# One core, a transformer block with routing: the last batch's outputs tile by tile, its last denominators in halves, its gates in the output weights

## The chip, the cores and the metric

The kernel runs on one core of one Trainium2 chip. The metric is device time in microseconds (us). The kernel before took 3617.36 us, the median of three runs that lay between 3617.17 and 3618.96 us.

## The reference, cut to what matters

The input x holds 8 batches of 1024 tokens with 256 features. A small matrix product of another input gives each batch six vectors of 256 numbers (sa, ca, ga, sb, cb, gb). All arithmetic is f32. In the reference's order:

```
ga = (2 * (ga >= 0) - 1) * maximum(abs(ga), 0.25)      # gb likewise
h  = layernorm(x) * (1 + ca) + sa
q, k, v of 16 heads of 64 features; softmax(q k' / 8) v; joined heads @ w_o
x  = x + ga * attention
h  = layernorm(x) * (1 + cb) + sb
logits = h @ router_w + router_b; scores = softmax over 8 experts
each expert takes the 512 tokens of all 8192 with its highest scores
h1 = relu(toks @ w1 + b1); eo = h1 @ w2 + b2; x = x + gb * (eo * score), added at the tokens
```

An expert cannot choose before the scores of all 8192 tokens are there. So everything after the attention of the last batch, up to its scores, lies ahead of the choice.

## The kernel before, in words

**Units.** Attention is cut into 128 units (NSU). Unit u is a batch b, a pair p of heads (8 pairs, NP) and a half h of the 512 queries (QB); the last two units, 126 and 127, are the two halves of the last pair of batch 7. A unit has 8 chunks c of 128 keys. For each chunk TensorE makes the scores (`scores_mm`, L367), ScalarE copies them to an SBUF tile with the tag "p" (16 buffers, L376), VectorE keeps a running maximum (L381) and later subtracts it (`subtract`, L426), ScalarE takes the exponential (`exp_of`, L429), and TensorE multiplies with the values (`values_mm`, L438); `values_out` (L447) copies the sum into the tile oT of the pair.

**Denominators.** GpSimd adds the eight chunks of a unit into one tile (`add_up`, L454 and L457), then TensorE sums that tile over its partitions with a matrix of ones (`den_mm`, L473), ScalarE copies the result (`den_store`, L481) and SyncE's queue carries it to DRAM. `den_load` fetches the two halves of a pair in a flat shape (L494), `den_inv` takes the reciprocal on VectorE (L499) and stores it (L501), `den_spread` spreads it over the partitions with two DMAs (L510), and `den_mul` multiplies oT with it (L517 or L519). For unit 127 alone no GpSimd addition is made: TensorE sums each of its eight chunks directly, in between the value products, into pd_last.

**Order.** The program is written out by hand in steps g, four to a unit; each engine and each DMA queue carries out its instructions in program order. `at(g, where, f, ...)` files a function under a step and one of the places "load", "m1", "post", "pool" and "m2" of it; `run` calls them. Values lag scores by six steps (LAG), so unit 127 is in g = 514 to 517. The denominators of unit u come at 4u + 12 in "m2".

**The end of the attention.** After the loop the store, the load, the reciprocal and the spread of the last pair are issued in one go, for both halves (units 126 and 127) together, and after them on the same SyncE queue the loads of the vectors of the last batch (mods, L777) and of its x (xs, L782). Eight loads of the earlier pairs' attention (`last_load`, L644), 384 KB each, stand in steps 515 and 516.

```
        for t in range(NT):
            for p in range(NP - 1):
                ...
        den_mul(b, NP - 1)
        for t in range(NT):
            add_pair(t, NP - 1, at_hand[b, NP - 1][:, t * P : (t + 1) * P])
        for s in range(NT + 5):
            if s < NT:
                out_add(b, s, pos[s])
            if 1 <= s < NT + 1:
                out_norm(b, s - 1)
            ...
```

The output product of the last batch (L797) thus runs over the first seven pairs of all eight token tiles t, then over the last pair of all eight, and only then come the sums, norms and router steps of the tiles. Per tile `out_add` multiplies the product by the gate (L558), adds x (L559), stores the row, and takes the statistics (L116, L117). `rstd_of` takes the inverse deviation on GpSimd (L106, L108). `out_norm` subtracts and scales on VectorE (L571), then multiplies and adds on GpSimd (L572, L573). For two tiles at a time `out_turn` transposes on TensorE (eight half-wide products a pair of tiles, L585) with a copy on ScalarE (L590), `out_route` makes the logits (L600, L605, L607), `out_exp` the exponentials (L615), `out_score` the scores (L622, L623, L626), and `out_store` copies the scores into the table of all tokens on GpSimd (L633) and stores the rows (L634).

**After it.** The whole table of scores is transposed (L883) and copied (L887), a search in 15 steps finds each expert's threshold (L898 to L916), the positions are made, rows are gathered, and eight experts run.

Of the kernel before, what the change touches and what calls it, by code (L numbers as in the profile page):

```python
# [28 lines left out]
F32 = mybir.dt.float32  # L29
# [3 lines left out]
ALU = mybir.AluOpType  # L33
# [4 lines left out]
P = 128  # L38
# [4 lines left out]
def adaln_block(  # L43
# [203 lines left out]
    def at(g, where, f, *args):  # L247
        steps.setdefault((g, where), []).append((f, args))
# [219 lines left out]
    def den_mm(pd, src, start=True, stop=True):  # L468

        for j in range(2):  # L470
            for i in range(2):
                r = (2 * j + i) * 32
                nc.tensor.matmul(  # L473
                    pd[r : r + 32, :], ones[:, :32], src[:, j, i * QH : (i + 1) * QH],
                    start=start, stop=stop, tile_position=(0, r),
                )

    def den_store(u, pd):
        b, p, h = unit(u)
        den = small.tile([P, QH], F32, tag="den", name=f"den{u}", bufs=2)  # L480
        nc.scalar.copy(den, pd)  # L481
        if h == 0:
            den_d[b, p] = dram.tile([2, S], F32, name=f"den_d{b}_{p}")
        nc.sync.dma_start(
            den_d[b, p][:, h * QB : (h + 1) * QB].rearrange("j (i q) -> j i q", i=2),
            den[::32, :],
        )


    dens = {}  # L490
# [1 line left out]
    def den_load(b, p):  # L492
        dens[b, p] = small.tile([P, 2 * S // P], F32, tag="dq", name=f"dq{b}_{p}", bufs=2)
        nc.sync.dma_start(  # L494
            dens[b, p], den_d.pop((b, p)).rearrange("j s -> (j s)").rearrange("(p c) -> p c", p=P)
        )
# [16 lines left out]

    def den_mul(b, p):
        oT = oTs.pop((b, p))
        if (b, p) == (B - 1, NP - 1):
            nc.vector.tensor_mul(oT, oT, dens.pop((b, p)))  # L517
        else:
            nc.gpsimd.tensor_tensor(oT, oT, dens.pop((b, p)), ALU.mult)  # L519
        if (b, p) in at_hand:  # L520
            at_hand[b, p] = oT
        else:
            nc.sync.dma_start(oT_d[b][p], oT)


    o_x, o_h, o_t = {}, {}, {}
# [49 lines left out]
    def out_turn(pool, b, t, tag="mm"):  # L576

        n = f"{b}_{t}"
        pt = pool.tile([P, 2, KC, P], F32, tag=tag, name=f"pth{n}")
        for i in range(2):  # L580
            h2 = o_h[b, t + i]
            for k in range(KC):
                for m in range(2):
                    c0 = k * P + m * N
                    nc.tensor.matmul(  # L585
                        pt[m * N : (m + 1) * N, i, k, :], h2[:, c0 : c0 + N], ident,
                        start=True, stop=True,
                    )
# [47 lines left out]
    def gates(b):  # L636
        nc.sync.dma_start(
            rows_d[b * S : (b + 1) * S, ROW:], gb_d[b : b + 1, :].to_broadcast([S, D])
        )

    def last_load(t):
        b = B - 1
# [56 lines left out]
    for u in range(NSU):  # L699
        at(4 * u + 4, "m1", max_rows, u)  # L700
        if u < NSU - 1:
            at(4 * u + 12, "m2", den_out, u)
    for b in range(B):
        at(64 * b + 30, "load", gates, b)
    for i in range(2):
        at(2 + i, "m2", mod_rows, i)
    for t in range(NT):
        at(4 * NSU + (3 if t < NT // 2 else 4), "load", last_load, t)

    with tc.manual_schedule():  # L710
        first_loads()
        late_loads()
        mod_silu()
        ln_first(0)
        ln_first(1)
        ln_norm(0, 0)
        mod_columns()
        for t in range(2, NT // 2):
            ln_first(t)
            ln_norm(0, t - 1)  # L720
        ln_norm(0, NT // 2 - 1)
        for t in parts_of:
            nc.vector.memset(t, 0.0)

        nc.gpsimd.memset(steps_of, 0)
        nc.gpsimd.iota(steps_of[:, 14, :], pattern=[[1, 4]], base=0, channel_multiplier=0)
        for s in range(14):
            nc.vector.tensor_scalar(
                steps_of[:, s, :], steps_of[:, 14, :], 28 - 2 * s, None, op0=ALU.logical_shift_left
            )  # L730
        g = -1
        while g < 4 * NSU + LAG or steps:
            u, gm = divmod(g, 4)
            run(g, "load")
# [12 lines left out]
            run(g, "m1")  # L747
            run(g, "post")
            for uc in late:
                exp_of(*uc)  # L750
            u1, gm1 = divmod(g - LAG, 4)
            if 0 <= u1 < NSU:
                for c in (2 * gm1, 2 * gm1 + 1):
                    values_mm(u1, c)
                    if u1 == NSU - 1:
                        if c == 0:
                            pd_last = ps_s.tile([P, QH], F32, tag="s", name="pd_last")
                        den_mm(pd_last, probs.pop((u1, c)), start=(c == 0), stop=(c == NT - 1))
# [12 lines left out]
        b = B - 1  # L771
        den_store(NSU - 1, pd_last)
        den_load(b, NP - 1)
        den_inv(b, NP - 1)
        den_spread(b, NP - 1)
        mods[b] = work.tile([P, 3, D], F32, tag="mod", name=f"mod{b}", bufs=1)
        nc.sync.dma_start(  # L777
            mods[b].rearrange("p m d -> p (m d)"), mod_d[b : b + 1, :].to_broadcast([P, 3 * D])
        )
# [9 lines left out]
        for pool, tag, n in (  # L789
            (ps_s, "s", 2), (ps_b, "less", 2), (ps_m, "mm", 1), (ps_av, "av", 1), (ps_s, "s", 2)  # L790
        ):
# [3 lines left out]
        def add_pair(t, p, src):  # L795
            for m in range(2):
                nc.tensor.matmul(  # L797
                    pos[t][m * N : (m + 1) * N, :], src[:, m * N : (m + 1) * N],
                    wo[:, p, :], start=(p == 0), stop=(p == NP - 1),
                )  # L800

        for t in range(NT):
            for p in range(NP - 1):
                if p < NP - 2:
                    add_pair(t, p, o_t[b, t][:, p, :])
                else:
                    add_pair(t, p, at_hand[b, p][:, t * P : (t + 1) * P])
        den_mul(b, NP - 1)
        for t in range(NT):
            add_pair(t, NP - 1, at_hand[b, NP - 1][:, t * P : (t + 1) * P])  # L810
        for s in range(NT + 5):
            if s < NT:
                out_add(b, s, pos[s])
            if 1 <= s < NT + 1:
                out_norm(b, s - 1)
            if s % 2 == 0 and 2 <= s < NT + 2:
                out_turn(*((ps_s, b, 0, "s") if s == 2 else (ps_m, b, s - 2)))
            if s % 2 and 3 <= s < NT + 3:
                out_route(ps_b, b, s - 3, tag="less")
                out_exp(b, s - 3)  # L820
            if s % 2 == 0 and 4 <= s < NT + 4:
                out_score(b, s - 4)
                out_store(b, s - 4)
    assert not steps, sorted(steps)
    attn.close()

# [283 lines left out]
```

## Time and profile before

| what | value |
|---|---|
| median of three runs | 3617.36 us |
| the profiled execution's own time | 3616.66 us |
| its span | 3614.9 us |
| TensorE busy | 96% of the span |
| VectorE, GpSimd, ScalarE busy | 80%, 74%, 67% |
| last value product's copy of the attention (L447) starts | 3213.17 us into the span |
| last scores copied into the table (L633) | 3271.52 us, for 0.33 us |
| first gathered rows asked for (L1007) | 3345.61 us |

The profiled execution took 1.76 us more than its span. All times inside the span are counted from its start. In the timeline a row gives start, length, engine, line and operation, then what is written and read, and in brackets how long the engine sat idle and what released it. PEld is the weight load of TensorE, SPq the issuing of DMAs on SyncE's queue. The rows of TensorE count two or four hardware passes for one f32 product.

### The profile page before, as it was taken

How to read it: one execution, taken by the hardware profiler on the slowest of the kernel's cores; microseconds unless marked ns; L12 is line 12 of the kernel's file. 1: busy time of each engine (PE TensorE's matmuls, PEld its weight loads, DVE VectorE, ACT ScalarE, POOL GpSimd, SP SyncE). 2: the span in 40 equal slices, each digit the busy share in tenths (PEclk: the TensorE clock that was granted, in tenths of full speed). 3: DMA queues.
4: the chain of work that ended last, by engine and by line, in shares of the span. 5: the costliest groups of instructions: out<-in, count | busy, mean ns of one | idle time of the engine just before them, and what ended most of it. 6: DMA issues, size and time to landing. Idle time of an engine off the chain costs nothing. (4 is left out here: it accounts for less than half of the span.)

```text
span 3614.9 us, 54207 instructions
## 1 busy us (share of the span) xinstructions
PE 3458.4 (96%) x20622; PEld 1456.3 (40%) x20622; DVE 2898.9 (80%) x3641; ACT 2439.8 (67%) x2988; POOL 2660.0 (74%) x1537
## 2 busy tenths in 40 slices
PE   7999999999999999999999999999999999982898
PEld 3333333343433443344433434334334344342565
DVE  5888888888888888888888888888888888857442
ACT  4777777777777777777777777777777777730111
POOL 2778777887788887977888788877888877851332
PEclk9999999999999999999999999999999999995999
DMA  3010012011111113111211112011201112133332
GB/s 77 13 42 31 25 32 67 29 45 45 59 50 35 51 49 64 31 39 51 61 46 44 41 44 62 30 52 48 67 29 45 45 59 49 51 87 121 94 100 41
DMA packets 189652, 185.39 MB, mean 51 GB/s; under 512 B 48952, under 2 KB 167240, under 8 KB 189264
## 3 DMA queue, kind: packets, MB, share of 16 engines
q1 hardware_dynamic: 173616, 160.29, 15.5%
q0 software_dynamic: 7168, 12.72, 1.7%
q10 hardware_dynamic: 8608, 8.92, 0.8%
q8 instruction: 162, 2.65, 0.3%
q14 instruction: 98, 0.80, 0.1%
HBM read 127.06 MB, written 63.21 MB: 53 GB/s over the span
## 5 line engine op out<-in xcount | busy, mean ns | idle before, releaser
L457 POOL TENSOR_TENSOR acc<-acc,p 128x1024 f32<-128x1024 f32 x762 | 1806.6, 2371 | 361.2 <-ACT p L429 328.1
L376 ACT COPY p<-s 128x1024 f32<-128x1024 f32 x1024 | 997.2, 1020 | 417.8 <-PE s L367 407.7
L426 DVE TENSOR_TENSOR p<-p,less 128x1024 f32<-128x1024 f32 x1024 | 1206.8, 1210 | 32.5 <-PE less L423 30.0
L381 DVE TENSOR_TENSOR top<-top,s 128x1024 f32<-128x1024 f32 x768 | 936.9, 1220 | 276.5 <-ACT p L376 236.2
L429 ACT ACTIVATE p<-p 128x1024 f32<-128x1024 f32 x1024 | 1042.8, 1058 | 73.7 <-DVE p L426 73.4
L367 PE MATMUL s<-qk,qk 64*128 64x512 f32 x4096 | 1025.1, 612 | 34.0 <-DVE parts L404 31.0
L438 PE MATMUL av<-p,v 128*64 128x512 f32 x4096 | 967.1, 593 | 1.8 <-ACT oT L447 1.8
L367 PEld LDWEIGHTS s<-qk,qk 64*128 64x128 f32 x4096 | 358.7, 186 | 527.8 <-issue 241.2
L332 PE MATMUL pq<-hT,wq 128*64 128x512 f32 x2048 | 498.4, 608 | 2.7 <-ACT v L354 2.1
L438 PEld LDWEIGHTS av<-p,v 128*64 128x64 f32 x4096 | 280.5, 137 | 461.4 <-issue 366.2
L454 POOL TENSOR_TENSOR acc<-p,p 128x1024 f32<-128x1024 f32 x127 | 301.8, 2376 | 178.0 <-ACT p L429 178.0
L332 PEld LDWEIGHTS pq<-hT,wq 128*64 128x64 f32 x2048 | 124.8, 136 | 342.4 <-issue 210.8
L349 PE MATMUL pv<-wq,hT 128*64 128x256 f32 x2048 | 249.3, 385 | 0.7 <-ACT qk L337 0.7
L1035 ACT ACTIVATE h<-ph,b_sb 128x512 f32<-128x512 f32 x64 | 44.1, 689 | 274.7 <-PE ph L1031 274.7
L396 DVE TENSOR_REDUCE tt<-tt 128x8 f32<-128x1024 f32 x128 | 157.4, 1230 | 69.6 <-PE tt L388 69.5
L548 PE MATMUL po<-wo,ot 128*64 128x256 f32 x1792 | 205.7, 382 | 0.0
L349 PEld LDWEIGHTS pv<-wq,hT 128*64 128x64 f32 x2048 | 135.6, 136 | 153.3 <-issue 65.9
L381 DVE TENSOR_TENSOR top<-p,s 128x1024 f32<-128x1024 f32 x128 | 155.8, 1217 | 14.5 <-ACT p L376 14.5
L388 PEld LDWEIGHTS tt<-ident,top 128*128 128x128 f32 x1024 | 109.6, 140 | 106.6 <-DVE top L381 105.8
L519 POOL TENSOR_TENSOR oT<-oT,rb 128x1024 f32<-128x1024 f32 x63 | 150.1, 2382 | 3.0 <-DMA rb<-rden_d 3.0
L548 PEld LDWEIGHTS po<-wo,ot 128*64 128x64 f32 x1792 | 123.6, 137 | 66.1 <-issue 9.4
L388 PE MATMUL tt<-ident,top 128*128 128x128 f32 x1024 | 139.9, 280 | 2.6 <-DVE top L381 2.6
(166 smaller groups left out, 2357.3 us busy)
## 6 DMA issues: line engine op xcount, KB each, us to landing
rb<-rden_d SPq DMA_DIRECT2D x128, 256.0 KB
oT_d<-oT SPq DMA_DIRECT2D x62, 512.0 KB
ot<-oT_d SPq DMA_DIRECT2D x56, 512.0 KB
rows_d<-row SPq DMA_DIRECT2D x64, 132.0 KB
rows_d<-gb_d SPq DMA_DIRECT2D x8, 1024.0 KB
w<-in_L_ffn_w_dram ACTq DMA_DIRECT2D x8, 1024.0 KB
w<-in_L_ffn_w_dram SPq DMA_DIRECT2D x8, 1024.0 KB
lnx<-in_L_attn_inputs_dram SPq DMA_DIRECT2D x28, 256.0 KB
```

The costliest lines, as they stand in the source:

```text
L332: nc.tensor.matmul(pq[m * N : (m + 1) * N, :], wq_of(k, a, 2 * p + m), hTs[b][:, k, sl], start=(k == 0), stop=(k == KC - 1),)
L349: nc.tensor.matmul(pv[m * N : (m + 1) * N, i, :], hTs[b][:, k, t0 : t0 + N], wq_of(k, 2, 4 * g, 4), start=(k == 0), stop=(k == KC - 1),)
L367: nc.tensor.matmul(ps[:, j, :], kt[r, c * P : (c + 1) * P], qt[r, h * QB : (h + 1) * QB], start=True, stop=True,)
L376: nc.scalar.copy(probs[u, c], ps)
L381: nc.vector.tensor_tensor(tops[u], probs[u, 0] if c == 1 else tops[u], ps, ALU.max)
L388: nc.tensor.transpose(turned[u][:, 4 * j + t, :], top[:, j, t * P : (t + 1) * P], ident)
L426: nc.vector.tensor_tensor(probs[u, c], probs[u, c], less[u], ALU.add)
L429: nc.scalar.activation(probs[u, c], probs[u, c], AF.Exp)
L438: nc.tensor.matmul(avs[u][j * N : (j + 1) * N, :], v[:, c, hh * N : (hh + 1) * N], pT[:, j, :], start=(c == 0), stop=(c == NT - 1),)
L454: nc.gpsimd.tensor_tensor(sums[u], pts[0], pts[1], ALU.add)
L457: nc.gpsimd.tensor_tensor(sums[u], sums[u], pt, ALU.add)
L548: nc.tensor.matmul(po[m * N : (m + 1) * N, :], ot[:, p, m * N : (m + 1) * N], wo[:, p, :], start=(p == 0), stop=(p == NP - 1),)
```

## The change

It touches the denominators of the last pair, the end of the attention, and the output of the last batch; the other seven batches' code is as it was.

- **Sums of unit 127.** Chunks 0 to 3 are added on GpSimd (`add_up` now also runs for unit 127 at its first two steps). Chunks 4 to 7 and that sum are summed by TensorE after the last value product, in a tile of another PSUM pool.
- **Halves.** Each half of the last pair has a DRAM tile, a load, a reciprocal, a store, a spread and a product of its own (`last_load_den`, `last_inv`, `last_mul`). The denominators of unit 126 come at step 515 instead of 516; their load is at 516, their reciprocal, store and spread at 517. Those of unit 127 follow the loop, behind the loads of xs.
- **Gates.** `last_mods` loads the vectors of the last batch at step 510. `last_gates` multiplies the output weights wo by the gate in two VectorE operations at step 516; `add_x` then has no product.
- **Order.** Token tiles 0 to 3 get pairs 0 to 6, then pair 7. Tiles 4 to 7 follow with all eight pairs each, and the sums, norms and router steps are put among them by a list.
- **Engines.** The product and the sum of the norm are on VectorE for odd tiles and on GpSimd for even ones. The transposes of the last batch are four whole ones for a pair of tiles instead of eight half ones.

```diff
@@ den_store
+        if (b, p) == (B - 1, NP - 1):
+            dst = den_d[b, p, h] = dram.tile([2, QB], F32, name=f"den_d{b}_{p}_{h}")
...
+    def last_load_den(h):
+        d = last_d[h] = small.tile([P, 2 * QB // P], F32, tag="dq", name=f"dq_last{h}", bufs=2)
+        nc.sync.dma_start(
+            d, den_d[B - 1, NP - 1, h].rearrange("j s -> (j s)").rearrange("(p c) -> p c", p=P)
+        )
+    def last_inv(h):
+        nc.vector.reciprocal(last_d[h], last_d[h])
+        rd = dram.tile([2, QB], F32, name=f"rden_last{h}")
+        nc.sync.dma_start(
+            rd.rearrange("j s -> (j s)").rearrange("(p c) -> p c", p=P), last_d[h]
+        )
+        t = last_d[h] = work.tile([P, QB], F32, tag="p", name=f"rb_last{h}", bufs=PB)
+        for j in range(2):
+            nc.sync.dma_start(
+                t[j * N : (j + 1) * N, :], rd[j : j + 1, :].to_broadcast([N, QB])
+            )
+    def last_mul(h):
+        half = oTs[B - 1, NP - 1][:, h * QB : (h + 1) * QB]
+        nc.vector.tensor_mul(half, half, last_d[h])
@@ out_turn
+                if b == B - 1:
+                    nc.tensor.transpose(pt[:, i, k, :], h2[:, k * P : (k + 1) * P], ident)
+                    continue
...
+    def last_gates():
+        n = NP // 2
+        for i in range(2):
+            w = wo[:, i * n : (i + 1) * n, :]
+            nc.vector.tensor_tensor(
+                w, w, mods[B - 1][:, 0, :].unsqueeze(1).to_broadcast([P, n, D]), ALU.mult
+            )
@@ the plan
-            at(4 * u + 12, "m2", den_out, u)
+            at(4 * u + (12 if u < NSU - 2 else 11), "m2", den_out, u)
+    at(4 * NSU - 2, "load", last_mods)
+    at(4 * NSU + 4, "load", last_load_den, 0)
+    at(4 * NSU + 4, "pool", last_gates)
+    at(4 * NSU + 5, "post", last_inv, 0)
@@ the loop
                     values_mm(u1, c)
-                    if u1 == NSU - 1:
-                        if c == 0:
-                            pd_last = ps_s.tile([P, QH], F32, tag="s", name="pd_last")
-                        den_mm(pd_last, probs.pop((u1, c)), start=(c == 0), stop=(c == NT - 1))
-                if u1 < NSU - 1:
+                if u1 < NSU - 1 or gm1 < 2:
                     add_up(u1, gm1)
@@ after the loop (the loads of xs stay in front)
+        pd_last = ps_m.tile([P, QH], F32, tag="mm", name="pd_last")
+        for c in range(4, NT):
+            den_mm(pd_last, probs.pop((NSU - 1, c)), start=(c == 4), stop=False)
+        den_mm(pd_last, sums.pop(NSU - 1), start=False)
+        den_store(NSU - 1, pd_last)
+        last_load_den(1)
+        last_inv(1)
...
+        half = NT // 2
+        for t in range(half):
+            add_pairs(t, 0, NP - 1)
+        last_mul(0)
+        for t in range(half):
+            add_pairs(t, NP - 1, NP)
+        last_mul(1)
+        for f, *args in (
+            (add_x, 0), (add_x, 1), (norm, 0), (add_pairs, 4, 0, NP), (add_x, 2), (norm, 1),
+            (add_x, 3), (norm, 2), (add_pairs, 5, 0, NP), (turn, 0), (add_x, 4), (norm, 3),
+            (route, 0), (norm, 4), (add_pairs, 6, 0, NP), (turn, 2), (score, 0), (add_x, 5),
+            (norm, 5), (route, 2), (add_pairs, 7, 0, NP), (turn, 4), (add_x, 6), (norm, 6),
+            (score, 2), (route, 4), (add_x, 7), (norm, 7), (score, 4), (turn, 6), (route, 6),
+            (score, 6),
+        ):
+            f(*args)
```

Here `add_x(t)` adds x to the product, stores the row and takes the statistics and the inverse deviation; `norm(t)` is the norm with its product and sum; `turn`, `route` and `score` call the functions named above on tiles t and t + 1.

More of the change, by code (lines that the diff above doesn't have):

```diff
@@ L481, in den_store @@
         nc.scalar.copy(den, pd)
[L482 to L487, printed above, removed]
+        if (b, p) == (B - 1, NP - 1):
+            dst = den_d[b, p, h] = dram.tile([2, QB], F32, name=f"den_d{b}_{p}_{h}")
+        else:
+            if h == 0:
+                den_d[b, p] = dram.tile([2, S], F32, name=f"den_d{b}_{p}")
+            dst = den_d[b, p][:, h * QB : (h + 1) * QB]
+        nc.sync.dma_start(dst.rearrange("j (i q) -> j i q", i=2), den[::32, :])
     dens = {}
@@ L515, in den_mul @@
         oT = oTs.pop((b, p))
[L516 to L519, printed above, removed]
+        nc.gpsimd.tensor_tensor(oT, oT, dens.pop((b, p)), ALU.mult)
         if (b, p) in at_hand:
@@ L523, in den_mul @@
             nc.sync.dma_start(oT_d[b][p], oT)
+    last_d = {}
+    def last_load_den(h):
[17 more added lines that the diff above has]
+        nc.vector.tensor_mul(half, half, last_d[h])
     o_x, o_h, o_t = {}, {}, {}
@@ L639, in gates, with last_mods @@
         )
+    def last_mods():
+        b = B - 1
+        mods[b] = work.tile([P, 3, D], F32, tag="mod", name=f"mod{b}", bufs=1)
+        nc.sync.dma_start(
+            mods[b].rearrange("p m d -> p (m d)"), mod_d[b : b + 1, :].to_broadcast([P, 3 * D])
+        )
[5 more added lines that the diff above has]
+                w, w, mods[B - 1][:, 0, :].unsqueeze(1).to_broadcast([P, n, D]), ALU.mult
+            )
     def last_load(t):
@@ L771, in adaln_block @@
         b = B - 1
[L772 to L779, printed above, removed]
         for i in range(2):
@@ L786, in adaln_block @@
                 o_x[b, 4 * i + t] = xs[:, t : t + 1, :]
+        pd_last = ps_m.tile([P, QH], F32, tag="mm", name="pd_last")
[5 more added lines that the diff above has]
+        last_inv(1)
         pos = []
         for pool, tag, n in (
-            (ps_s, "s", 2), (ps_b, "less", 2), (ps_m, "mm", 1), (ps_av, "av", 1), (ps_s, "s", 2)
+            (ps_s, "s", 2), (ps_s, "s", 2), (ps_b, "less", 2), (ps_m, "mm", 1), (ps_av, "av", 1)
         ):
@@ L793, in adaln_block @@
             pos += [po[:, i, :D] for i in range(n)]
[L795 to L799, printed above, removed]
-                )
[L802 to L823, printed above, removed]
+        def add_pairs(t, p0, p1):
+            for p in range(p0, p1):
+                src = (
+                    o_t[b, t][:, p, :] if p < NP - 2
+                    else (at_hand[b, p] if p == NP - 2 else oTs[b, p])[:, t * P : (t + 1) * P]
+                )
+                for m in range(2):
+                    nc.tensor.matmul(
+                        pos[t][m * N : (m + 1) * N, :], src[:, m * N : (m + 1) * N],
+                        wo[:, p, :], start=(p == 0), stop=(p == NP - 1),
+                    )
@@ new lines, in add_x, with norm @@
+        def add_x(t):
+            x1 = o_x[b, t]
+            nc.vector.tensor_add(x1[:, 0, :], x1[:, 0, :], pos[t])
+            nc.sync.dma_start(out[b, t * P : (t + 1) * P, :], x1[:, 0, :])
+            mv = stats_of(small, x1, 1, f"b{b}_{t}")
+            o_h[b, t] = mv, rstd_of(small, mv, 1, f"b{b}_{t}")
+        def norm(t):
+            mv, rs = o_h[b, t]
+            row = small.tile([P, ROW], F32, tag="row", name=f"row{b}_{t}", bufs=6)
+            h2 = row[:, :D]
+            nc.vector.tensor_scalar(
+                h2, o_x.pop((b, t))[:, 0, :], mv[:, 0, 0:1], rs, op0=ALU.subtract, op1=ALU.mult
+            )
+            eng = nc.vector if t % 2 else nc.gpsimd
+            eng.tensor_tensor(h2, h2, mods[b][:, 2, :], ALU.mult)
+            eng.tensor_tensor(h2, h2, mods[b][:, 1, :], ALU.add)
+            o_h[b, t] = row
@@ new lines, in turn, with route, score @@
+        def turn(t):
+            out_turn(ps_s, b, t, tag="s")
+        def route(t):
+            out_route(ps_s, b, t, tag="s")
+        def score(t):
+            out_exp(b, t)
+            out_score(b, t)
+            out_store(b, t)
+        half = NT // 2
[14 more added lines that the diff above has]
+            f(*args)
```

## The prediction

> **What bounds the kernel now.** On the page's slices TensorE is busy nearly throughout, except late in the span, where the granted clock falls to half. I read the busy time by stretch there (engine busy times with counts, granted clock, DMA share, GB/s):
>
> ```profile
> 3200.00:3225.00 25.00, 24.44 (x210) 10.73 (x212) 6.97 (x12) 8.33 (x13) 4.34 (x4) 1.00 0.70 173
> 3225.00:3250.00 25.00, 19.27 (x186) 12.74 (x182) 8.62 (x21) 0.59 (x1) 6.98 (x13) 0.90 0.29 87
> 3250.00:3275.00 25.00, 11.15 (x100) 7.75 (x100) 15.09 (x53) 3.74 (x11) 15.82 (x43) 0.50 0.44 152
> ```
>
> First TensorE is full, then it is half idle while no other engine is full either: a chain of hand-overs. The timeline shows the links:
>
> ```profile
> 3213.17 0.59 ACT L447 COPY oT<-av 128x512 f32<-128x512 f32 x1 [2.15 <-PE av L438]
> 3215.28 1.17 SPq L484 DMA_DIRECT2D den_d<-den  x2
> 3219.24 0.32 SPq L494 DMA_DIRECT2D dq<-den_d  x1
> 3220.76 0.25 DVE L499 RECIPROCAL dq<-dq 128x16 f32<-128x16 f32 x1 [13.97 <-DMA dq<-den_d]
> 3222.49 1.15 SPq L510 DMA_DIRECT2D rb<-rden_d  x2
> 3227.82 1.23 DVE L517 TENSOR_TENSOR oT<-oT,rb 128x1024 f32<-128x1024 f32 x1 [6.81 <-DMA rb<-rden_d]
> 3237.41 4.05 PE L797 MATMUL po_last<-wo,oT 128*64 128x256 f32 x36
> 3238.93 0.42 DVE L558 TENSOR_TENSOR at<-po_last,mod 128x256 f32<-128x256 f32 x1 [9.88 <-PE po_last L797]
> 3259.68 0.41 DVE L558 TENSOR_TENSOR at<-po_last,mod 128x256 f32<-128x256 f32 x1
> 3271.52 0.33 POOL L633 COPY scores<-row 128x8 f32<-128x8 f32 x2 [1.17 <-DVE row L626]
> ```
>
> The values end at 3213.2. The denominators' round trips end at 3229.05 (L517), early, since TensorE has other pairs to multiply until 3237. So TensorE sets the first tile's start (3238.93), the chain the last scores' end (3271.85). The search follows, waiting for all scores; it is unchanged, so the time won is 3271.85 less the new end of the scores.
>
> **What the Trainium skill says.** "TensorE: Matmul & The Clock Gate", Part 1: one idle window of about 3.4 us halves the clock, one busy window restores it. The trace agrees: TensorE ran out of products at 3241.5; eight passes of L585 took 0.66 us at 3243.95 and 1.12 us at 3246.98. "DMA: Bandwidth & Descriptors", Queues, rings and completion order: descriptors on an engine's ring are consumed in order. Agreed: the small den_d, issued by 3216.45 behind loads that kept the DMA at 290 GB/s until 3218, let its reader issue at 3219.24 only. "SBUF — State Buffer", Who interferes with whom: a VectorE operation with two SBUF inputs contends with GpSimd's reads. L559 took 0.42 us alone and 0.72 beside GpSimd.
>
> **Part 1, sums of unit 127.** Value and sum alternate at 1.58 us a chunk. Alone, two chunks of values take 1.77 us (steps at 3196.41 and 3198.18). From 3200.56, with unit 126's sum (0.7 us) moved up between them, products could end by 3208.4; but the last exponential ends at 3207.88, so I take 3208.8, 4.3 us sooner. Five sums of 0.57 us follow: TensorE is free at 3211.7. So the output product starts 1.9 us before 3213.6. GpSimd gains three additions of 2.37 us behind its last one (ends 3201.64): 3208.8, in time for the fifth sum; then L633 (0.33) and pair 6's product (2.37), which slips from 3210.2 to 3211.5. TensorE reads that at 3211.7 + 2.6 = 3214.3: cover 2.8 us.
>
> **Part 2, gates.** Two 128x1024 products on VectorE: 1.23 us each (L517) to twice that beside GpSimd. VectorE is idle from 3206.8 (last subtraction) until the reciprocal, so they end at 3209.3 to 3211.7; wo is read from 3211.7. At worst GpSimd loses 2.4 us, and pair 6 comes at 3213.9, still covered. Price 0, at most 0.5 us. Removed: eight times 0.46 us of L558 with its gap. Moving the load of mods to step 510 costs nothing: SyncE then waits 16 us for a denominator, and the last reader of the earlier mods ended at 3177.5.
>
> **Part 3, halves.** The two halves share SyncE's queue, so I add up its issues. The eight L644 loads start at 3204.45. After four (3208.1) comes unit 126's den_d, ready at 3205.3; the other four end at 3213.6 (1.3 us each at the ring's pace). Then the load of half 0: it lies behind 3.67 MB that 290 GB/s drain by 3217.2, so its reciprocal runs at 3218.0. The row stores (L634), queued behind that load, are issued meanwhile; on VectorE only the reciprocal of half 1 and the two products stand behind this new wait, and TensorE waits for those. Spread of half 0: 3218.0 + 1.73 (L499 to L510 before) = 3219.7 to 3220.9; xs to 3221.8; den_d of unit 127 to 3222.3. It is behind 0.26 MB of spread and 1.05 MB of xs: about 4.9 us from 3220.4, so it lands at 3226.0. Load and reciprocal take 1.55 (3219.24 to 3220.76): 3227.6. VectorE has the reciprocal of half 1 queued ahead of the product of half 0, so that product waits for it: 3227.9 to 3228.6. Spread of half 1 is issued at 3229.35; no trace row shows a half spread. Bounds: 1.9 us (its issue and 0.26 MB at 280 GB/s) to 5.3 (the whole, contended spread, 3222.49 to 3227.82). I take 2.5: product 3231.9 to 3232.6.
>
> **Part 4, TensorE.** Tiles 0 to 3 with seven pairs: 4 x 3.02 us (28 passes a tile, from L797's starts), 3211.7 to 3223.9. Then it waits for 3228.6: a new stall of 4.7 us. It is longer than the skill's window, so half clock is likely; bounds are 0 and all the rest at half. I take 2.5 us at half rate, a loss of 1.25. Four last products (4 x 0.43), then four tiles of 3.45 us with turns and routes between.
>
> **Part 5, the chain.** VectorE begins add_x 0 at 3232.6, not 3238.93, because half 1's product stands ahead of it. Its durations: add, stats and aggregate 1.1 us; norm 0.41; product and sum of an odd tile 1.05 (between 0.46 alone and 0.72 each); logits 0.38; scores 0.76; inverse deviation 0.84 on GpSimd; even products 1.55 on GpSimd; copy 0.59 on ScalarE, exponentials 0.5. I laid the in-order queues out with these and 0.05 us for a hand-over. Milestones: add_x 3 ends 3238.9; TensorE finishes tile 5 at 3238.5, turn 0 at 3239.1, route 0 at 3240.5, tile 6 at 3244.0, tile 7 at 3249.4, turn 4 at 3250.5, route 4 at 3251.9. VectorE: add_x 7 is queued behind route 4's logits and ends at 3255.2, norm 7 at 3257.6. Turn 6 ends at 3258.3, route 6 at 3260.1 (half clock, L600's 1.03), scores at 3261.9, copy at 3262.3. A turn is now four whole transposes; L388 does eight in 1.09 us at full clock, so I count 0.55 a turn, twice that at half. Buffers hold nothing up: turn 0 and route 0 take the PSUM banks of tiles 0 and 1, and 2 and 3, and add_x 3 has read the last of these at 3238.9, before route 0; the rows of tiles 6 and 7 reuse those of 0 and 1, stored some 6 us earlier.
>
> The sum: 3271.85 - 3262.3 = 9.55 us less. The profiled execution took 3616.66 (span 3614.9 and 1.76 around it), so 3607.1; that execution lies 0.70 below the median of 3617.36. I forecast 3607.0.
>
> **The rivals.** *A quick chain*: small DMAs overtake the loads, the reciprocal of half 1 is done by 3224, there is no stall, products of half 1 end by 3227.8. The same layout ends at 3257.0: 14.8 less, about 3602. For it: steady-state den_d lands 1.35 us after issue (3155.33 to 3156.68). Against: den_d behind loads took 2.8.
>
> *A slow chain*: half 1's store or spread meets xs harder, its product ends at 3235.5. The layout then gives 3264.6 to 3266: 6 to 7 less, about 3610.3. For it: the spread before needed 5.3 us when xs stood behind it. Against: xs is here ahead and drained by then.
>
> *The clock stays low*, the case that ends slower. The stall's half clock never recovers, as TensorE then has gaps between tiles. All TensorE work after 3228.6 at half rate ends the layout at 3279.5, 7.7 later: 3624.3. It turns slower than before once half clock outlasts about 21 us of the chain (10.7 us lost). For it: half clock lasted from 3247 to beyond 3325. Against: there TensorE had 11.15 us of work in 25, here 3.45 us of products in one piece per tile.
>
> **How the numbers follow.** Forecast 0.55 (3604 to 3610), quick 0.14, slow 0.25, low clock 0.06. A measurement tells 0.2%, 7.2 us, from no change: the line is at 3610.1. Faster: 0.52 + 0.14 + 0.09 = 0.75. Slower by that much: half of the low clock, 0.03. Between: 0.22. The range runs from beyond the quick case, 3600.5, to beyond the slow one, 3612.
>
> **What would show it.** Last value product near 3208.8; first output product near 3211.7; a TensorE gap near 3224 ended by half 0's product near 3228.6; add_x 0 near 3232.6; add_x 7's start about 3 us behind tile 7; last L633-like copy near 3262, and the search as long as before. A gap of under 2 us, or add_x 0 before 3229 or after 3236, makes the forecast wrong.

## The result and the profile after

The changed kernel took 3610.71 us, the median of 15 runs between 3608.85 and 3612.04. The kernel before, on the same chip, took 3617.83 us (3615.75 to 3619.16). The ratio is 0.998, with a 95% interval of 0.9972 to 0.9988: 7.1 us less. The forecast was 3607.0, with a range of 3600.5 to 3612.0; its most likely case, 3604 to 3610, was missed by 0.7 us.

The profiled execution after took 3609.12 us, its span 3607.4. Busy time by stretch of it, in the columns that the prediction gave:

```profile
3200.00:3225.00 25.00, 22.50 (x176) 10.52 (x178) 10.93 (x14) 7.93 (x12) 12.99 (x7) 0.93 0.71 184
3225.00:3250.00 25.00, 19.93 (x184) 12.37 (x182) 12.68 (x35) 1.56 (x4) 9.01 (x18) 0.93 0.20 65
3250.00:3275.00 25.00, 8.83 (x72) 5.68 (x68) 16.50 (x64) 2.54 (x8) 7.76 (x29) 0.66 0.68 242
```

VectorE now works 12.7 us in the second stretch, where it had 8.6: norm and router have moved in among the products. TensorE was granted 0.93 of its clock in the first stretch, where the kernel before had 1.00; e1 and e2 below show why. The timeline of the same execution has the links that answer to those of before:

```profile
3211.42 0.58 ACT L447 COPY oT<-av 128x512 f32<-128x512 f32 x1 [1.80 <-PE av L438]
3213.79 1.18 SPq L529 DMA_DIRECT2D dq_last<-den_d  x1
3214.61 2.81 PE L844 MATMUL po_last<-wo,ot 128*64 128x256 f32 x24
3218.81 0.20 DVE L534 RECIPROCAL dq_last<-dq_last 128x8 f32<-128x8 f32 x1 [8.02 <-DMA dq_last<-den_d]
3221.11 1.10 SPq L541 DMA_DIRECT2D rb_last<-rden_last  x2
3222.31 1.08 SPq L817 DMA_DIRECT2D xs<-in_L_attn_inputs_dram  x2
3223.49 0.52 SPq L489 DMA_DIRECT2D den_d<-den  x1
3227.63 0.33 SPq L529 DMA_DIRECT2D dq_last<-den_d  x1
3229.18 0.20 DVE L534 RECIPROCAL dq_last<-dq_last 128x8 f32<-128x8 f32 x1 [10.17 <-DMA dq_last<-den_d]
3229.36 0.69 DVE L547 TENSOR_TENSOR oT<-oT,rb_last 128x512 f32<-128x512 f32 x1
3229.41 0.34 SPq L536 DMA_DIRECT2D rden_last<-dq_last  x1
3230.11 3.38 PE L844 MATMUL po_last<-wo,oT 128*64 128x256 f32 x16 [3.19 <-DVE oT L547]
3231.97 1.10 SPq L541 DMA_DIRECT2D rb_last<-rden_last  x2
3235.51 0.69 DVE L547 TENSOR_TENSOR oT<-oT,rb_last 128x512 f32<-128x512 f32 x1 [5.46 <-DMA rb_last<-rden_last]
3236.12 0.42 DVE L852 TENSOR_TENSOR xs<-xs,po_last 128x256 f32<-128x256 f32 x1
3256.41 0.41 DVE L852 TENSOR_TENSOR xs<-xs,po_last 128x256 f32<-128x256 f32 x1
3263.97 0.33 POOL L660 COPY scores<-row 128x8 f32<-128x8 f32 x2 [0.47 <-DVE row L653]
```

The chain through SyncE's queue is the one that the prediction laid out: half 0's spread at 3221.11, then xs, then unit 127's den_d, its load, its reciprocal, its store and its spread; half 0's product stands behind half 1's reciprocal; TensorE stops for it (the 3.19 in brackets), and add_x 0 follows half 1's product. But that product comes at 3235.51, not at 3231.9.

The start of this stage shifts by up to 2.3 us between the profiled executions, so I count from the start of the copy (L447) of unit 126's values, t0: 3199.94 before, 3199.60 after. Entries are starts, except for the end. "Products" are those of half 0 and half 1 of the last pair with their denominators, "end" is the end of the last copy of scores. From there to the end of the span it is 343.05 us before and 343.1 after: search and experts have not moved.

| kernel | values' last copy | products | add_x 0 | add_x 7 | end |
|---|---|---|---|---|---|
| before | 13.23 | 27.88 (both) | 38.99 | 59.74 | 71.91 |
| forecast | 9 | 28, 32 | 32.66 | | 62.36 |
| after | 11.82 | 29.76, 35.91 | 36.52 | 56.81 | 64.70 |

The stage is 7.21 us shorter, 2.47 by the start of add_x 0 and 4.74 behind it. The forecast had 9.55.

### The profile page after: what moved, and what is told of

It reads as the page before. It is cut to its first block, busy times and chain, and to the rows that moved or that the text cites. A ratio compares the mean times of both kernels' runs of the same rounds, so it can differ in the third digit from the quotient of the medians.

```text
span 3607.4 us, 54072 instructions
## 1 busy us (share of the span) xinstructions
PE 3452.8 (96%) x20550; PEld 1452.2 (40%) x20550; DVE 2902.8 (80%) x3645; ACT 2436.4 (68%) x2988; POOL 2662.1 (74%) x1532
```

## The experiments

Each is the changed kernel with one edit, except e13, which is the kernel before with one part of the change. Stage times are from t0 of each one's own profile. "Before it" is the median of the kernel before, measured beside that experiment; the ratio is formed with it. After, as above, has 11.82, 29.76 and 35.91, 36.52, 64.70.

| kernel | values | products | add_x 0 | end | median | before it | ratio (95%) |
|---|---|---|---|---|---|---|---|
| e1 | 8.47 | 30.22, 36.20 | 36.81 | 65.00 | 3612.06 | 3617.22 | 0.9986 (0.9979 to 0.9993) |
| e2 | 9.11 | 29.82, 35.78 | 36.39 | 64.58 | 3610.55 | 3617.22 | 0.9982 (0.9975 to 0.9989) |
| e3 | 12.06 | 26.42, 31.75 | 32.36 | 60.55 | 3605.88 | 3617.22 | 0.997 (0.9958 to 0.9981) |
| e4 | 11.98 | 29.75, 35.83 | 36.44 | 64.61 | 3611.47 | 3617.22 | 0.9984 (0.9977 to 0.9991) |
| e5 | 11.71 | 30.00, 35.13 | 35.74 | 68.06 | 3612.31 | 3617.43 | 0.9985 (0.9978 to 0.9992) |
| e6 | 11.69 | 29.39, 35.59 | 36.20 | 67.03 | 3614.07 | 3617.43 | 0.9991 (0.9984 to 0.9997) |
| e9 | 11.19 | 29.79, 36.02 | 32.09 | 63.97 | 3609.45 | 3617.43 | 0.9978 (0.9969 to 0.9987) |
| e8 | 8.47 | 26.39, 34.21 | 28.91 | 57.30 | 3603.6 | 3617.43 | 0.9961 (0.9947 to 0.9974) |
| e11 | 11.67 | 27.9, 28.5 | 29.9 | 60.39 | 3606.84 | 3617.14 | 0.997 (0.9958 to 0.9982) |
| e12 | 8.47 | 27.13, 35.20 | 29.9 | 59.77 | 3604.54 | 3617.14 | 0.9966 (0.9954 to 0.9979) |
| e13 | 13.23 | 27.53 | 39.0 | 69.80 | 3615.27 | 3617.14 | 0.9997 (0.9988 to 1.0005) |
| e14 | 11.82 | 27.5, 28.2 | 29.4 | 60.03 | 3606.5 | 3617.22 | 0.9971 (0.9959 to 0.9984) |

### e1 and e2: why the values did not end sooner

The values' copy is at 11.82 where I had about 9. A step between the subtractions had grown: the scores of the batch before (L653), two tiny operations. Answers on this line and on GpSimd's additions, after (duration min, median and max in ns, first and last start):

```profile
L653 DVE TENSOR_SCALAR row<-ex,rd x2: 219/1265/2311, 3203.8 to 3206.1; 128x8 f32<-128x8 f32 x2
```

```profile
L457 POOL TENSOR_TENSOR acc<-acc,p x2: 2362/2365/2368, 3203.7 to 3206.2; 128x1024 f32<-128x1024 f32 x2
```

The first of the two scores took 2.31 us: it began just behind an addition on GpSimd and ended with it. These additions are the ones that the change gave to unit 127.

The delay of the values has a second part. The subtractions, and with them the exponentials, came later, TensorE waited 2.23 us for one, and its granted clock was 0.50 from 3210.0 to 3213.4:

```profile
3208.54 2.84 PE L438 MATMUL av<-p,v 128*64 128x512 f32 x8 [2.23 <-ACT p L429]
3211.31 2.94 PE L473 MATMUL pd_last<-p,ones 128*32 128x256 f32 x32
```

The 32 passes of the second row took 1.93 us in e1, where the clock stayed at 1.00.

e1 moves the scores one step on, behind the last subtractions; e2 takes the additions away and lets TensorE sum all eight chunks behind the values.

```diff
# e1
-                    at(g + 2, "post", out_score, b, t - 1)
+                    late = b == B - 2 and t == NT - 1
+                    at(g + (3 if late else 2), "post", out_score, b, t - 1)
# e2
-                if u1 < NSU - 1 or gm1 < 2:
+                if u1 < NSU - 1:
                     add_up(u1, gm1)
...
-        for c in range(4, NT):
-            den_mm(pd_last, probs.pop((NSU - 1, c)), start=(c == 4), stop=False)
-        den_mm(pd_last, sums.pop(NSU - 1), start=False)
+        for c in range(NT):
+            den_mm(pd_last, probs.pop((NSU - 1, c)), start=(c == 0), stop=(c == NT - 1))
```

> Edit: in the changed kernel the score step of the last two tiles of batch 6 comes one step later, behind the last subtractions of unit 127. Theory (shared port): in the changed kernel its two small VectorE products took 2.44 us because GpSimd now adds chunks of unit 127 at that moment, and the last subtractions waited for it. Then the copy behind the last value product starts about 2 us sooner (3209.4 instead of 3211.4 on the profile's clock), and the end of the scores (3264.3) moves by under 0.3 us, since TensorE waits 3.2 us for the first half's product anyway. Rival (the additions slow something else, or TensorE is late by itself): the copy stays at 3211.4.

> Edit: no GpSimd additions for unit 127; TensorE sums all eight chunks behind the values. Theory (the round trips of the second half set the end): the small score products are back at 0.36 us, the values' copy starts at 3209.4, the sums take 4.6 us instead of 2.9, the first output product starts at about 3214, and the end of the scores stays at 3264.3 within 0.3 us; the whole time is the same. Rival (the start of the output product sets the end): the end moves with the first product's start.

In e2 the same line takes a tenth of that:

```profile
L653 DVE TENSOR_SCALAR row<-ex,rd x2: 226/228/230, 3205.4 to 3205.5; 128x8 f32<-128x8 f32 x2
```

In e1 the wait is still there, but behind the subtractions, where no subtraction waits for it (timeline of e1):

```profile
3207.95 2.55 DVE L653 TENSOR_SCALAR row<-ex,rd 128x8 f32<-128x8 f32 x2
3209.93 0.59 ACT L447 COPY oT<-av 128x512 f32<-128x512 f32 x1 [1.21 <-PE av L438]
```

The values end 3.35 us sooner in e1 and 2.71 in e2, and the end of the stage does not move (65.00 and 64.58 against 64.70). So the cause is shown, and so is its price for the time: nothing that can be measured. TensorE, done sooner, waits longer for half 0's denominators: 7.53 us in e1 and 5.68 in e2, against 3.19.

### e3, e4 and e8: what held half 1 up

e3 loads xs at step 510, into tiles of the tag "ot"; the den_d of unit 127 then has no 1 MB of loads before it.

```diff
+    def last_x():
+        b = B - 1
+        for i in range(2):
+            xs = work.tile([P, 4, D], F32, tag="ot", name=f"xs{i}")
+            nc.sync.dma_start(
...
+    at(4 * NSU - 2, "load", last_x)
```

e4 keeps the order and writes and reads the halves as 64 rows of 16 numbers, twice the piece of before.

```diff
-        d = last_d[h] = small.tile([P, 2 * QB // P], F32, tag="dq", name=f"dq_last{h}", bufs=2)
+        d = small.tile([P, 2 * QB // N], F32, tag="dq", name=f"dq_last{h}", bufs=2)
+        d = last_d[h] = d[:N, :]
...
-            rd.rearrange("j s -> (j s)").rearrange("(p c) -> p c", p=P), last_d[h]
+            rd.rearrange("j s -> (j s)").rearrange("(p c) -> p c", p=N), last_d[h]
```

> Edit: the two loads of the last x (1 MB) are issued at step 510 into buffers of the earlier output stage, no longer between the two halves' transfers. Theory (the round trips set the end): the store of unit 127's sums is issued 1.1 us sooner and has no megabyte ahead of it, so the reciprocal of half 1 runs near 3225.4 instead of 3229.2, the gap of TensorE (3.2 us) is gone and its clock stays full, add_x 0 starts near 3232.4 instead of 3236.1, and the end of the scores comes 3 to 4 us sooner; the time falls by as much. Rival (after add_x 0 TensorE or the hand-overs are the bound, the start is absorbed): the end moves by under 1.5 us.

> Edit: the half reciprocals are loaded and stored as 64 partitions of 16 numbers (64 bytes a piece, as in the whole pair before) instead of 128 partitions of 8 (32 bytes). Theory (small pieces are slow to store): the step from the reciprocal's store to the spread's issue falls from 2.07 and 2.56 us to about 1.45 in both halves, add_x 0 starts 1.5 us sooner and the end of the scores comes 1.5 us sooner. Rival (the row stores and the x loads in the rings make it slow): both stay above 2 us and nothing moves.

Half 1's chain in the timeline of e3, to be laid beside the one of after:

```profile
3222.26 1.10 SPq L541 DMA_DIRECT2D rb_last<-rden_last  x2
3223.46 0.52 SPq L489 DMA_DIRECT2D den_d<-den  x1
3225.43 0.32 SPq L529 DMA_DIRECT2D dq_last<-den_d  x1
3227.20 0.20 DVE L534 RECIPROCAL dq_last<-dq_last 128x8 f32<-128x8 f32 x1 [6.86 <-DMA dq_last<-den_d]
3227.43 0.32 SPq L536 DMA_DIRECT2D rden_last<-dq_last  x1
3228.87 1.11 SPq L541 DMA_DIRECT2D rb_last<-rden_last  x2
3232.65 0.69 DVE L547 TENSOR_TENSOR oT<-oT,rb_last 128x512 f32<-128x512 f32 x1 [4.66 <-DMA rb_last<-rden_last]
```

add_x 0 comes 4.16 us sooner and the end 4.15: one for one. By differences of the issue times, link by link, e3 less after: spread of half 0 to den_d 1.20 for 2.38 (xs is no longer issued between); den_d to its load 1.97 for 4.14 (xs is no longer ahead in the rings); load to reciprocal 1.77 for 1.55; store to spread 1.44 for 2.56; spread to product 3.78 for 3.54. The first two, 3.35 us, are xs. The store's 1.12 is not: in after the DMA engines had emptied by then. The stretches of the timeline around it, after, show a DMA share (second number from the end) of 0.98 only up to 3227:

```profile
3225.00:3227.00 2.00, 1.92 (x18) 1.00 (x14) 0.00 (x0) 0.00 (x0) 0.00 (x0) 1.00 0.98 327
3227.00:3229.00 2.00, 0.00 (x0) 0.00 (x0) 0.00 (x0) 0.00 (x0) 0.00 (x0) 1.00 0.08 16
3229.00:3231.00 2.00, 0.89 (x6) 0.59 (x8) 0.87 (x2) 0.00 (x0) 0.00 (x0) 0.87 0.06 6
3231.00:3233.00 2.00, 2.00 (x12) 1.11 (x10) 0.00 (x0) 0.00 (x0) 0.00 (x0) 0.50 0.00 0
```

The other kernels confirm the price of xs and leave the store open. den_d to its load took 4.14 to 4.57 us in all seven kernels that keep xs ahead of it, and 1.97 and 1.94 in the two that don't (e3, e8). Half 1's store to its spread took 2.38 to 2.70 in six of the seven and 1.49 in the seventh (e5), 1.44 in e3 and 2.38 in e8: it goes with no edit. e4's bigger pieces gave 2.38, and half 0's store, 1.89, so the size of a piece isn't it either. For comparison, the store of the whole pair at this place took 1.44 to 1.46 us to its spread in all five kernels that have one (before, e11 to e14), and of the 63 stores of whole pairs in the loop of after 55 took 1.39 to 1.48, the other eight 1.80 to 3.44. What stretches the stores of the halves so often stays open. The lines of e8, with xs early too, show both findings, 1.94 and 2.38:

```profile
3223.59 0.52 SPq L489 DMA_DIRECT2D den_d<-den  x1
3225.53 0.32 SPq L529 DMA_DIRECT2D dq_last<-den_d  x1
3227.58 0.32 SPq L536 DMA_DIRECT2D rden_last<-dq_last  x1
3229.96 1.11 SPq L541 DMA_DIRECT2D rb_last<-rden_last  x2
```

And the spread itself: 3.45 to 3.78 us from issue to product for half 1, in the kernels where nothing else holds the product back. In after nothing moved from 3231 to 3233 (0 GB/s), so most of the wait is not bytes.

### e5 and e13: the gates

e5 puts the gate back into add_x. e13 does the reverse to the kernel before: it loads the vectors at step 510, multiplies wo at step 516, and leaves the products out of the last batch's sums.

```diff
# e5
-            nc.vector.tensor_add(x1[:, 0, :], x1[:, 0, :], pos[t])
+            tmp = small.tile([P, D], F32, tag="at", name=f"at{b}_{t}", bufs=2)
+            nc.vector.tensor_mul(tmp, pos[t], mods[b][:, 0, :])
+            nc.vector.tensor_add(x1[:, 0, :], x1[:, 0, :], tmp)
...
-    at(4 * NSU + 4, "pool", last_gates)
# e13, on the kernel before
+    at(4 * NSU - 2, "load", last_mods)
+    at(4 * NSU + 4, "pool", last_gates)
...
+        if b == B - 1:
+            nc.vector.tensor_add(x1[:, 0, :], x1[:, 0, :], po)
```

> Edit: the gate is again multiplied into each tile's product on VectorE (0.46 us with its gap, eight times), and not into the output weights. Theory (after add_x 0 VectorE's queue is nearly full and sets the pace): the end of the scores comes 2.5 to 3.7 us later. Rival (the hand-overs and TensorE set the pace): under 1 us later. The start of add_x 0 does not move in either.

> Edit: the kernel before with one part of the change: the vectors of the last batch loaded at step 510 and the gates multiplied into the output weights, nothing else. Theory (the chain after the first tile is paced by VectorE): the end of the scores comes 2.5 to 3.5 us sooner than the 71.9 us of the kernel before. Rival (the chain is paced by hand-overs and GpSimd): under 1 us.

e5's end is 3.36 us later than after's, though its add_x 0 was 0.78 sooner: from there to the end it takes 4.14 us more, a little above the sum of eight products of 0.46 us (3.7 us). So the pace is set in VectorE's queue, as Part 5 had it, though not by its work alone: VectorE is busy for 19.63 of these 28.18 us in after and for 22.30 of 32.32 in e5, and in after it waits 0.94 to 0.95 us at each of the last three norms for the inverse deviation from GpSimd. On the kernel before the same part gives 2.11 by the profile, less than the 2.5 to 3.5 expected; the median, 1.87 lower, has an interval that includes no change.

### e6 and e9: the order

e6 issues all products of tiles 4 to 7 ahead of the list. e9 moves half 1's product on VectorE behind add_x 2, so that add_x 0 need not wait for it.

```diff
# e6
+        for t in range(half, NT):
+            add_pairs(t, 0, NP)
         for f, *args in (
-            (add_x, 0), (add_x, 1), (norm, 0), (add_pairs, 4, 0, NP), (add_x, 2), (norm, 1),
+            (add_x, 0), (add_x, 1), (norm, 0), (add_x, 2), (norm, 1),
...
# e9
-        last_mul(1)
         for f, *args in (
-            (add_x, 0), (add_x, 1), (norm, 0), (add_pairs, 4, 0, NP), (add_x, 2), (norm, 1),
+            (add_x, 0), (add_x, 1), (norm, 0), (add_x, 2), (last_mul, 1), (add_pairs, 4, 0, NP), (norm, 1),
```

> Edit: the output products of tiles 4 to 7 stand ahead of all transposes and router products on TensorE, the rest of the list as it is. Theory (the interleaving is worth something because the transposes do not wait for all products): tile 7's product ends near 3250 instead of 3252, but turn 0 comes near 3250 instead of 3240.8, VectorE waits for route 0 until about 3252 instead of 3245.7, and the end of the scores comes 4 to 6 us later. Rival (the order is worth nothing, the gain is all from the earlier start and the gates): within 1 us.

> Edit: on VectorE the product of half 1 stands behind add_x 0, add_x 1, norm 0 and add_x 2, nothing else is changed. Theory (VectorE's wait of 5.5 us for the spread of half 1 is on the path, since add_x 0 is queued behind it): add_x 0 starts near 3231.5 instead of 3236.1 and the end of the scores comes 2 to 4 us sooner, what remains being TensorE's pace. Rival (TensorE's tile 4 waits for the same product, so nothing is won): under 1 us.

e6 ends 2.33 us later than after: turns and routes behind four tiles' products wait for TensorE, but less than I expected. e9 starts add_x 0 4.43 us sooner and ends only 0.73 sooner: half 1's product, and with it tile 4, come when they came. add_x 0's wait behind it was therefore not a cost of its own; the denominators of half 1 were.

### e11, e14: no halves

e11 takes the halves out: the last pair has one load, reciprocal, store and spread again, with xs behind the spread as in the kernel before, and the product on VectorE is still made per half. e14 is the same with xs at step 510.

```diff
-        if (b, p) == (B - 1, NP - 1):
-            dst = den_d[b, p, h] = dram.tile([2, QB], F32, name=f"den_d{b}_{p}_{h}")
...
-    at(4 * NSU + 4, "load", last_load_den, 0)
-    at(4 * NSU + 5, "post", last_inv, 0)
...
-        last_load_den(1)
-        last_inv(1)
+        den_load(b, NP - 1)
+        den_inv(b, NP - 1)
+        den_spread(b, NP - 1)
```

> Edit: the changed kernel with the halves undone: one store tile, one load, reciprocal, store and spread for the whole last pair after the loop, the x loads behind the spread; gates in the weights, GpSimd sums and the interleaved order stay. Theory (the halves delay the last product, because half 1's chain starts behind half 0's and behind the x loads): both products are done near 30 us after the copy of unit 126's values, where half 1's is done at 36.5 in the changed kernel, add_x 0 starts near 31, and the end of the scores comes 4 to 6 us sooner (59 to 61 instead of 64.7). Rival (the halves are worth what they were meant for): no sooner, or later than 64.7.

> Edit: the changed kernel with one chain for the whole last pair and the x loads early, its list as it is; against the run that has the halves and the x loads early (both products done at 32.4, end of the scores at 60.55 us after the copy of unit 126's values). It separates the halves from the place of the x loads. Theory (without the x loads between them the halves are worth nothing, the second half's chain follows the first's): products done between 28 and 30, end at 58 to 60.5. Rival (the halves save time once nothing stands between them): end later than 60.8.

In the timeline of e11 both products run as one piece, TensorE stops 1.38 us instead of 3.19, and add_x 0 follows:

```profile
3229.25 1.29 DVE L543 TENSOR_TENSOR oT<-oT,rb 128x512 f32<-128x512 f32 x2 [6.39 <-DMA rb<-rden_d]
3231.29 0.42 DVE L847 TENSOR_TENSOR xs<-xs,po_last 128x256 f32<-128x256 f32 x1 [0.75 <-DMA xs<-in_L_attn_inputs_dram]
```

e11 ends 4.31 us before after, 11.52 before the kernel before. So the rest of the change is worth some 11.5 us by the profile (10.3 by the medians), and the halves with xs between them gave 4.3 back. Of these parts the gates have a price, measured on the changed kernel (e5, 3.36), and the interleaved products (e6, 2.33); the start of the first tiles, the whole transposes and the share of VectorE and GpSimd have no run of their own. With xs early, halves (e3, 60.55) and whole (e14, 60.03) differ by half a microsecond, and their medians (3605.88 and 3606.5) the other way. In this order halves as such win nothing that can be measured, for half 0's product at 26.42 in e3 is 1.1 sooner than the pair's in e14 and half 1's 3.6 to 4.2 later.

### e8 and e12: a better order

e8 takes e3's and e1's edits and a list in which norms 0 and 1 stand ahead of half 1's product, which has its place before tile 4's last pair. e12 is e8 with the whole pair of e11.

```diff
-        last_mul(1)
         for f, *args in (
+            (add_x, 0), (add_x, 1), (norm, 0), (norm, 1), (add_pairs, 4, 0, NP - 1),
+            (last_mul, 1), (add_pairs, 4, NP - 1, NP), (add_x, 2), (add_x, 3), (turn, 0),
+            (norm, 2), (norm, 3), (add_pairs, 5, 0, NP), (add_x, 4), (route, 0), (norm, 4),
+            (add_pairs, 6, 0, NP), (add_x, 5), (score, 0), (norm, 5), (turn, 2),
+            (add_pairs, 7, 0, NP), (add_x, 6), (norm, 6), (route, 2), (turn, 4), (add_x, 7),
+            (norm, 7), (route, 4), (score, 2), (turn, 6), (score, 4), (route, 6), (score, 6),
```

> Edit: the x loads early, the score step of batch 6 one step later, the product of half 1 behind add_x 0, add_x 1, norm 0 and norm 1, and add_x 7 no longer behind the logits of tiles 4 and 5. Theory (three serial waits are left in the changed kernel: x loads between the halves, VectorE behind the spread, add_x 7 behind route 4): the stretch from the copy of unit 126's values (3199.6) to the end of the scores falls from 64.7 to 54 to 57 us and the whole time to about 3600. Rival (VectorE is already full): it falls only by the 4 us that the early x loads gave, to about 60.5, and the time to 3606.

> Edit: the same undoing of the halves in the reordered kernel (x early, score step later, reordered list). Theory: the second product is done near 27 instead of 34.9 us after the copy, TensorE's tile 4 waits no longer, and the end of the scores comes at 54 to 56 us instead of 57.3; the time at about 3601. Rival (VectorE's own work is the bound there): the end stays at 57 within 0.5 us.

e8 ends at 57.30, 7.4 before after, and takes 3603.6 us: 0.9961 of the kernel before, the best of all, though just short of the 54 to 57 and 3600 expected. It changes three things at once, and which move of the list gives the 3.25 us beyond e3 is not separated. e12 was expected to be at least as good and ends at 59.77. In its timeline TensorE waits 4.51 us for the pair, 3.74 in e8, and tile 5's six pairs take 4.50 us, where e8 had 2.81:

```profile
3229.25 3.35 PE L844 MATMUL po_last<-wo,oT 128*64 128x256 f32 x16 [4.51 <-DVE oT L543]
3237.30 0.65 PE L844 MATMUL po_last<-wo,oT 128*64 128x256 f32 x4 [1.69 <-DVE oT L543]
3238.47 4.50 PE L844 MATMUL po_last<-wo,ot 128*64 128x256 f32 x24
```

Tile 5 starts 0.99 us later from t0 than in e8 and takes 1.69 more: after the wait of 1.69 us in the second row the granted clock was 0.50 from 3238.95 to 3242.4, while e8, with a wait of 1.17, kept 1.00 there. So most of the 2.47 us by which e12 ends later may be the clock; no run takes it away. In both, half 1's product stands on VectorE behind norm 1, so that the whole pair's early spread is of no use to it (35.2 in e12, 34.2 in e8). Their medians lie 0.9 us apart, and the intervals of their ratios overlap: which of the two is better is not settled by time.

## Why the prediction was right, and where it missed

The direction, the place and most of the mechanism held: products among the router steps, a chain through SyncE's queue, a new stall of TensorE, VectorE's add_x 0 behind half 1's product. The forecast's own stop sign, add_x 0 after 3236, was crossed by 0.12 us, so the forecast's own case did not come. The slow rival's time, 3610.3, is what came, with half 1's product from 3235.51 to 3236.20 where that rival had its end at 3235.5; but its reason, half 1's store or spread meeting xs, is not: the DMA engines were nearly idle then but for the spread's own bytes. That the number lies in the range is therefore in part luck.

**Part 1 was wrong and cost nothing.** It counted the additions' own time on GpSimd and not what they do to VectorE. "SBUF — State Buffer", Who interferes with whom, in the Trainium skill, says that a tensor_scalar on VectorE can need the port pair shared with GpSimd, and that whoever issues first holds it for the whole instruction. The traces agree: 2.31 us beside an addition of 2.36, 0.23 without. Output products began at 3214.61, 2.9 us behind the forecast; TensorE's stall shrank from 4.7 to 3.19, since half 0's product was late by less.

**Part 2** held in its price: the gates ran at 3208.45, beside other work. The removed products were worth 3.36 us (e5), on the kernel before 2.11 (e13).

**Part 3 failed, in its sizes.** add_x 0 was late by 3.86 us from t0. The terms, from start to start, as forecast and as measured: half 0's reciprocal at 18.06 and 19.21 from t0; reciprocal to spread 0, 1.73 and 2.30; spread 0 to den_d of unit 127, 2.1 and 2.38; den_d to reciprocal 1, 5.8 and 5.69; reciprocal to spread 1, 1.75 and 2.79; spread 1 to product, 2.55 and 3.54. Three are off by about a microsecond. For half 0's reciprocal I had the loads ahead of it drained by 3217.2; at 3218 the DMA engines still moved some 140 GB/s. For the last two I took the store's time from one row of before (L499 to L510), and put half a spread near the lower of my bounds, which counts its issue and its bytes. The runs show 3.45 to 3.78 us for half a spread, against 4.57 and 4.73 for the whole in e14 and e12 (e11, with xs behind it: 4.90). Half the bytes save about a fifth of the wait. What I did foresee, unit 127's den_d behind xs, took place: "DMA: Bandwidth & Descriptors", Queues, rings and completion order, says descriptors are consumed in order, and e3 and e8 show 2.2 us as its price, 3.35 with xs's issue. I listed it as a term and not as a thing that a different order avoids.

**Part 4.** "TensorE: Matmul & The Clock Gate", Part 1, gives an idle window of about 3.4 us; here 3.19 us of stall sufficed, and so did the 2.23 us ahead of 3208.54. The kernel before, which the prediction took as agreeing, had a gap of 2.49 us (3241.46 to 3243.95), and its clock fell at 3244.8, after eight more passes. After 1.38 us (e11) it stayed at 1.00. So the measurement decides: a gap well below the window can be enough. The 16 passes after the stall took 3.38 us, against 1.95 in e11 at full clock: 1.4 lost, where I had 1.25. But it lost nothing at the end: from add_x 0 to the end it is 28.18 us in after and 28.19 in e3, which had no such stall and full clock there. VectorE stands at half 1's product while TensorE is slow.

**Part 5** had 29.7 us from add_x 0 to the end, and 28.18 came: 1.5 better, 1.2 of it before add_x 7 (20.3 us behind add_x 0, forecast 21.5). Late by 3.86, quicker by 1.52: 2.34 us worse than forecast. That the second error took back part of the first was luck. With t0 0.34 earlier, 3607.1 becomes 3609.1 for the profiled execution, which took 3609.12. The rest of the miss is that the median lies 1.59 us above that execution, and before's only 0.70 in the three runs that the forecast rested on.

The *low clock* rival, the one that ends slower, is out: the clock is back at 1.00 by 3234 and stays there until 3257.8. The half clock after that falls on the last turn and route, for which the forecast had counted it.

## What to carry to other kernels

Splitting a chain of small round trips in two does not halve the waits: most of such a round trip here was not bytes, so the second half pays it again, and a large load issued between the two adds its own drain. Put loads that nobody needs yet long before such a chain, and count each link from several rows, not from one. An engine whose work ends sooner is worth only what stands behind it: check what it waits for next before counting a gain.

## What the runs showed of the hardware

- An operation on 128x8 numbers took 2.31 us on VectorE beside one addition on GpSimd, and 0.23 without it.
- Half a spread (256 KB to SBUF from 4 KB of DRAM) took 3.45 to 3.78 us from issue to use, the whole 4.57 to 4.73, with 1 MB of loads behind it 4.90 to 5.33.
- A store of 4 KB on nearly idle DMA engines took from 1.43 to 2.70 us to the next issue, in kernels with the same instructions around it; one of 8 KB at the same place took 1.44 to 1.46 in five kernels.
- TensorE's clock fell to half after stalls of 2.23 and 3.19 us (the changed kernel), 2.49 (before), and in e12 after 1.69 and 0.52 with 0.65 of work between; it stayed at 1.00 after 1.38 (e11), 1.17 (e8) and 0.97 (e14). In the changed kernel it was at half for 3.4 us both times, until 4.9 and 3.8 us after the work began again.
